# Blocks 2 and 3 of a fp32 RWKV kernel: the time norm on transposed tokens, and block 0's first v mix after its r mix

## The chip, the cores and the metric

The kernel runs on one core of one Trainium2 chip. The metric is the device time of one execution in microseconds (us), lower being better. One core has five engines that matter here: TensorE (PE, matrix products and transposes), VectorE (DVE), ScalarE (ACT), GpSimd (POOL, which here mostly issues DMA transfers) and SyncE (SP, which only issues DMA transfers). A transfer is issued by an engine's queue, in order, and lands some us later.

## The reference

2048 tokens of 512 features, fp32, pass through an RWKV block and then a gated FFN. Cut to what matters:

```python
x = x + attn(_layernorm(x))            # attn is the block below
# in the block, on its own input x:
h  = _layer_norm(x, ln1_g, ln1_b)
hh = _time_shift(h)                    # the token before
k = (h * tm_mk + hh * (1 - tm_mk)) @ Wk.T
v = (h * tm_mv + hh * (1 - tm_mv)) @ Wv.T
r = (h * tm_mr + hh * (1 - tm_mr)) @ Wr.T
x = x + sigmoid(r) * wkv(k, v, tm_first) @ Wo.T
h = _layer_norm(x, ln2_g, ln2_b)       # then the channel mix:
x = x + sigmoid((mixed by cm_mr) @ Wcr.T) * (silu((mixed by cm_mk) @ Wkey.T) @ Wval.T)
# outside the block:
x = x + ((silu(gate) * up) @ w_down.T) # gate, up from _layernorm(x) @ w_gate_up.T
```

The scan starts from an empty state for all tokens at once, so `wkv` is elementwise here. Two norms stand one behind the other ahead of k, v and r (the outer one and ln1); both come from the same mean and variance.

## The kernel before

**Tiling.** Tokens are worked in four blocks (`NB`) of 512 (`TB`), block 0 first. A token tile is 128 tokens on the partitions by 4x512; its turned form hT has features on the partitions, four chunks of 128 features by 512 tokens, plus one column for the token before the block. Products use halves of 256 tokens and, except those listed in `PLAIN` (L658, `plain_unit`), a Strassen scheme of seven products in place of eight (L556, `unit`): each needs sums of the operand's quarters (`sums_of`, DVE) and of the weight's quarters. A product's PSUM bank is copied out by ACT (accv at L576, u at L587, accx at L591) and added by DVE (`tt`, L385).

**Weight sums.** `prepare` (L144 to L160) loads four raw quarters by POOL's queue (L149), makes four sums with DVE (L385) and stores them to DRAM by POOL's queue (L160). `ring` (L163 to L165) loads each product's weight, raw or sum, by SP's queue into a ring of 12 tiles. A load made by `paced` waits for the latest matmul recorded before it, so that it isn't issued too early.

**The time norm.** `time_norm(b)` takes mean and variance per token on DVE (`moments`, L399 and L400), forms `rstd` and `both` (the scale of the two norms together), scales the tile to h (four DVE tensor_scalar, L389), transposes h by PE (`transposed`, 16 transposes at L441), and ACT evacuates each bank of four with ln1's gain and bias to hT (L453). Column 0 of hT is copied from `carry` before it and the last column saved after it (L449, L459). Block 0 has a version of its own, `first_block` (L810 to L844). `residual` (L742, ACT) makes the outer normalised x, which the block adds to.

**Mixes.** `mix` makes an operand of k, r or v from hT: per chunk ACT scales the shifted hT (L494) and DVE adds the scaled hT (L393); two shifted copies are made ahead of the first mixed one. The k product's results go through two ACT exponentials (L879, L880) and DVE (L389, L393).

**Order.** PE's, DVE's and ACT's instructions stand in the order in which the program records them. A planner does this recording: main programs such as `k_unit` and `up_unit` record the products one after the other, and between the products `tick` runs pieces of generators from two queues: of the front one of `hot` and the first three of `background`, the first that can go on is stepped until the time that its pieces are estimated to cost is spent. A `yield` ends a piece, and `yield 1` also waits for the next tick. A generator pushed with a condition starts when the condition holds; those behind it that have a condition then wait too. `later` puts a piece off by ticks. The order on SP and POOL is the tile framework's. `push_mix` (from L862) pushes a block's mixes with the condition that its norm is finished and an operand tile is free.

The main program (from L1270) begins:

```python
second_half = first_block()
for n in "rv":
    push_mix(0, n, time_mix(0, n))
credit[1] = 0.6
k_unit(0)
```

and, for each block b, records the gate product of its channel mix, then the out product of block b + 1, pushes `norm{b+2}`, and with the first `up_unit` of b pushes the mixes of block b + 2 and the channel norm of block b + 1. So the time norms of blocks 2 and 3 run beside products of blocks 0 and 1, at about 150 and 310 us.

Of the kernel before, what the change touches and what calls it, by code (L numbers as in the profile page):

```python
# [9 lines left out]
F32 = mybir.dt.float32  # L10
AF = mybir.ActivationFunctionType
ALU = mybir.AluOpType
# [3 lines left out]
P = 128  # L16
H = 512
NC = H // P
TB = 512
NT = TB // P  # L20
# [9 lines left out]
LN1G, LN1B, LN2G, LN2B, FIRST, MK, MV, MR, CK, CR = range(10)  # L30
NVEC = 10

WK, WV, WR, WO, WCR = range(5)

PLAIN = {(0, WK), (0, WR), (0, WV), (0, WO), (1, WK), (1, WR)}
WKEY = 5
WVAL = 9
# [23 lines left out]
def rwkv_ffn_kernel(  # L61
    ctx: ExitStack,
    tc: tile.TileContext,
    x: bass.AP,
    vecs: bass.AP,
    w: bass.AP,
    wd: bass.AP,
# [2 lines left out]
    nc = tc.nc  # L70
    ntok = x.shape[0]
    NB = ntok // TB
# [12 lines left out]
    dram = ctx.enter_context(tc.tile_pool(name="dram", bufs=1, space=bass.MemoryType.DRAM))  # L85
# [3 lines left out]
    htp = mixes.enter_context(tc.tile_pool(name="htp", bufs=2))  # L89
# [9 lines left out]
    def tok_tile(name):  # L99
        return tokp.tile([P, NT, H], F32, tag="tok", name=name)  # L100
# [103 lines left out]
    def cost(n, fixed=0.135, per=0.00107):  # L204
        spent[0] += max(0.17, fixed + per * n)
# [7 lines left out]
    def flush():  # L213
        while put_off:
            flush_one()
# [27 lines left out]
    finished = set()  # L243
# [68 lines left out]
    def push(name, gen, ready=None):  # L312
        background.append([ready, gen, name, False, background])
# [18 lines left out]
    ident = const.tile([P, P], F32, name="ident")  # L332
# [6 lines left out]
    pt = ps.tile([P, 2, HB], F32, tag="ps", name="warm")  # L339
# [27 lines left out]
    carry = {}  # L367
# [4 lines left out]
    def vcol(row, c):  # L372
        return vec[:, row, c : c + 1]
# [22 lines left out]
    def moments(src, mv):  # L396
        for t in range(src.shape[1]):
            st = small.tile([P, 6], F32, tag="st", name="st")
            nc.vector.bn_stats(st, src[:, t, :])  # L399
            nc.vector.bn_aggr(mv[:, t, :], st)  # L400
            cost(512)
            cost(0)
            yield

    def rsqrt(v, y, n, early=False):


        if early:
            nc.gpsimd.tensor_tensor(y, v, mhalf[:, :n], ALU.pow)
            for _ in range(n // NT):  # L410
                yield 1
            return
        a = small.tile([P, n], F32, tag=f"a{n}", name="a")
        yi = y.bitcast(I32)
        ts(yi, v.bitcast(I32), 1, None, ALU.logical_shift_right)
        ts(yi, yi, -1.0, float(0x5F3759DF), ALU.mult, ALU.add)
        yield
        for _ in range(3):
            stt(a, y, -0.5, y, ALU.mult, ALU.mult)
            tt(a, a, v, ALU.mult)  # L420
            stt(y, a, 1.5, y, ALU.add, ALU.mult)
            yield

    def scaled(src, dst, mv, rstd):
        for t in range(NT):
            ts(
                dst[:, t, :],
                src[:, t, :],
                mv[:, t, 0:1],
                rstd[:, t : t + 1],  # L430
                ALU.subtract,
                ALU.mult,
            )
            yield

    def transposed(h, evacuate):
        for c in range(NC):
            pt = bank()
            flat = pt.rearrange("p a b -> p (a b)")
            for t in range(NT):  # L440
                nc.tensor.transpose(  # L441
                    flat[:, t * P : (t + 1) * P], h[:, t, c * P : (c + 1) * P], ident
                )
            evacuate(c, flat)
            spent[0] += 0.4
            yield

    def shifted_norm(s, h, hT, g, b):
        nc.vector.tensor_copy(hT[:, :, 0:1], carry[s])  # L449
        cost(0)  # L450

        def evacuate(c, pt):
            nc.scalar.activation(  # L453
                hT[:, c, 1:], pt, AF.Identity, bias=vcol(b, c), scale=vcol(g, c)
            )

        yield from transposed(h, evacuate)
        yield 1
        nc.vector.tensor_copy(carry[s], hT[:, :, TB : TB + 1])  # L459
        cost(0)  # L460
# [11 lines left out]
    def op_free():  # L472
        return live_ops[0] < 3
# [236 lines left out]
    def product_of(b, n, name, sink, by_token, done=None, free=op_done):  # L710
        if (b, name) not in ops:
            flush()
        plain = (b, n) in PLAIN
        B = Lazy((b, name), plain)
# [18 lines left out]
    x1s, ops, hTs = {}, {}, {}  # L733

    def residual(b, xb, cols):

        x1 = tok_tile("x1")
        x1s[b] = x1
        for t, (mean, scale) in enumerate(cols):
            shift = small.tile([P, 1], F32, tag="shift", name="shift")  # L740
            stt(shift, mean, -1.0, scale, ALU.mult, ALU.mult)
            nc.scalar.activation(x1[:, t, :], xb[:, t, :], AF.Identity, bias=shift, scale=scale)  # L742
            spent[0] += 0.4
            yield

    def affine(var, mv):


        n = mv.shape[1]
        ts(var[:, :n], mv[:, :, 1], EPS, None, ALU.add)  # L750
        ts(var[:, n : 2 * n], mv[:, :, 1], 1.0 + EPS, EPS * EPS, ALU.mult, ALU.add)

    def time_norm(b):
        xb = xin.pop(b)
        mv = small.tile([P, NT, 2], F32, tag="mv", name="mv")
        yield from moments(xb, mv)
        var = small.tile([P, 2 * NT], F32, tag="var2", name="var2")
        affine(var, mv)
        two = small.tile([P, 2 * NT], F32, tag="two", name="two")
        yield from rsqrt(var, two, 2 * NT, b == 1)  # L760
        rstd, both = two[:, :NT], two[:, NT:]
        h = tok_tile("h")
        yield from scaled(xb, h, mv, both)
        hT = htp.tile([P, NC, TB + 1], F32, tag="hT", name="hT_a")
        hTs[b, "a"] = hT
        tails[b] = residual(b, xb, [(mv[:, t, 0:1], rstd[:, t : t + 1]) for t in range(NT)])
        if b == 1:
            yield 1
        yield 1
        yield from shifted_norm("a", h, hT, LN1G, LN1B)  # L770

    def first_block():

# [76 lines left out]
    tails = {}  # L850
# [7 lines left out]
    def time_mix(b, name):  # L858
        row, n = {"k": (MK, WK), "r": (MR, WR), "v": (MV, WV)}[name]
        yield from mix((b, name), hTs[b, "a"], row, (b, n) in PLAIN)  # L860

    def push_mix(b, name, gen):  # L862
        norm = f"normb{b}" if name in ("cr", "ck") else f"norm{b}"
        push((b, name, "t"), gen, lambda: norm in finished and op_free())

    qs = {}

# [38 lines left out]
    def v_unit(b):  # L906
# [5 lines left out]
        def done():  # L912
            hidden_sums((b, "g"), q, (b, WO) in PLAIN)

# [367 lines left out]
    for n in "rv":  # L1282
        push_mix(0, n, time_mix(0, n))
# [7 lines left out]
    for n in "krv":  # L1291
        push_mix(1, n, time_mix(1, n))
# [10 lines left out]
    for b in range(NB):  # L1303
# [9 lines left out]
        if nxt:  # L1313
            push(f"norm{b + 2}", time_norm(b + 2))
# [46 lines left out]
def _layout(inputs):  # L1361

    import numpy as np

    def get(name):
        return np.asarray(inputs["L0_" + name])

    x = np.ascontiguousarray(get("attn_x").reshape(-1, H))
    names = ["ln1_g", "ln1_b", "ln2_g", "ln2_b", "tm_first", "tm_mk", "tm_mv", "tm_mr", "cm_mk", "cm_mr"]
    vecs = np.stack([get("attn_" + n).reshape(NC, P).T for n in names], axis=1)  # L1370

    gu = get("ffn_w_gate_up")
    half = gu.shape[0] // 2
    gate, up = gu[:half], gu[half:]
    key, val, down = get("attn_Wkey"), get("attn_Wval"), get("ffn_w_down")
    blocks = [get("attn_" + n) for n in ("Wk", "Wv", "Wr", "Wo", "Wcr")]
    blocks += [key[j * H : (j + 1) * H] for j in range(4)]
    blocks += [val[:, j * H : (j + 1) * H] for j in range(4)]
    blocks += [gate[j * H : (j + 1) * H] for j in range(4)]
    blocks += [up[j * H : (j + 1) * H] for j in range(4)]  # L1380

    def quarter(m, i, j):
        q = m[i * HB : (i + 1) * HB, j * HB : (j + 1) * HB]

        return q.T.reshape(2, P, HB).transpose(1, 0, 2)

    w = np.stack(
        [
            np.stack([quarter(m, i, j) for i, j in ((0, 0), (0, 1), (1, 1), (1, 0))])
            for m in blocks  # L1390
        ]
    )
    def quarter_quarter(i, j, m, k):
        at = slice(i * HB + m * P, i * HB + (m + 1) * P)
        lo = j * HB + k * P

        q = [down[at, g * H + lo : g * H + lo + P].T for g in range(4)]
        return np.stack(q, axis=1).reshape(P, 4 * P)

    places = ((0, 0), (0, 1), (1, 1), (1, 0))  # L1400
    wd = np.stack(
        [np.stack([quarter_quarter(i, j, m, k) for m, k in places]) for i, j in places]
    )
    return {
        "x": x,
        "vecs": np.ascontiguousarray(vecs),
        "w": np.ascontiguousarray(w),
        "wd": np.ascontiguousarray(wd),
    }
# [19 lines left out]
```

## Time and profile before

| | |
|---|---|
| runs | 1241.83, 1241.83, 1243.77 us; median 1241.83 |
| the profiled execution | 1242.04 us, its span 1239.9 us |
| TensorE clock granted | 1.0 |
| PE busy by stretch (us of us) | 0 to 25: 22.45; 50 to 100: 50.00; 100 to 150: 49.59; 150 to 300: 150.00 |
| | 300 to 480: 180.00; 480 to 500: 19.80; 500 to 800: 300.00; 800 to 1240: 435.40 |
| DVE busy by stretch | 50 to 100: 38.16; 100 to 150: 37.48; 150 to 200: 36.59 |
| ACT busy by stretch | 50 to 100: 19.99; 100 to 150: 19.70; 150 to 200: 24.28 |
| share of DMA engines' time | 50 to 100: 0.72; 100 to 150: 0.88; 150 to 200: 0.68; 200 to 300: 0.86 |
| transposes of the norms (L441) | 16 records for a block's norm, 128x128 each, mean 0.27 us, at 150.7, 206.0, 309.6 and so on |

The profile is that of one execution, so its numbers are compared with its own time. A line of a timeline reads: start, length, engine, line, operation, output and inputs, count, and in brackets how long the engine had been idle and what ended that. A line of the waits reads: what waited, for whom, us in total, times, longest. A line of the windows reads: the stretch, then its length, and busy us and count of PE, PEld (weight loads), DVE, ACT and POOL, then PE's clock, the DMA share and GB/s. In the list of DMA issues the last column is us from issue to landing. The matmuls of PE overlap, so that a record is longer than the step from one to the next.

### The profile page before, as it was taken

How to read it: one execution, taken by the hardware profiler on the slowest of the kernel's cores; microseconds unless marked ns; L12 is line 12 of the kernel's file. 1: busy time of each engine (PE TensorE's matmuls, PEld its weight loads, DVE VectorE, ACT ScalarE, POOL GpSimd, SP SyncE). 2: the span in 40 equal slices, each digit the busy share in tenths (PEclk: the TensorE clock that was granted, in tenths of full speed). 3: DMA queues.
4: the chain of work that ended last, by engine and by line, in shares of the span. 5: the costliest groups of instructions: out<-in, count | busy, mean ns of one | idle time of the engine just before them, and what ended most of it. 6: DMA issues, size and time to landing. Idle time of an engine off the chain costs nothing.

```text
span 1239.9 us, 18124 instructions
## 1 busy us (share of the span) xinstructions
PE 1231.2 (99%) x6552; PEld 1105.0 (89%) x6552; DVE 704.8 (57%) x1307; ACT 356.9 (29%) x661; POOL 153.7 (12%) x278
## 2 busy tenths in 40 slices
PE   8999999999999999999999999999999999999998
PEld 7888888888888888888888888998899888998898
DVE  5877686487763758523542365556546365462466
ACT  5534352142631334212311232122221222112211
POOL 2232221222212222221100000000000000000000
PEclk9999999999999999999999999999999999999999
DMA  6768885898778887899756755895569845785576
GB/s 204 238 216 286 288 277 199 295 318 288 247 255 261 283 261 240 262 329 305 229 145 181 225 144 151 268 339 153 145 183 302 275 141 154 240 295 160 152 223 204
DMA packets 138983, 290.12 MB, mean 234 GB/s; under 512 B 17424, under 2 KB 18576, under 8 KB 137872
## 3 DMA queue, kind: packets, MB, share of 16 engines
q1 hardware_dynamic: 116448, 217.11, 57.4%
q0 software_dynamic: 21440, 70.27, 15.5%
q10 hardware_dynamic: 1008, 1.59, 0.3%
q8 instruction: 53, 0.87, 0.3%
q14 instruction: 34, 0.28, 0.1%
HBM read 246.96 MB, written 41.94 MB: 233 GB/s over the span
## 4 chain that ended last, share of the span: by engine, by line
PE 96%; ACT 1%; DVE 1%; DMA 1%; POOL 0%; issue 0%; DVEq 0%
PE ps L556 54%; PE ps L1160 14%; PE accv L556 11%; PE accx L556 11%; PE ps L658 6%; PE ps L441 1%; DMA raw<-in_wd 1%; ACT mix L494 0%; DMA x<-in_x 0%; ACT mix L823 0%; ACT hT_a L815 0%; DVE mix L393 0%; DVE resid L385 0%; DVE r L385 0%; POOL raw L149 0%
## 5 line engine op out<-in xcount | busy, mean ns | idle before, releaser
L556 PE MATMUL ps<-zT,w 128*128 128x256 f32 x1280 | 289.5, 379 | 0.0
L556 PEld LDWEIGHTS ps<-zT,w 128*128 128x128 f32 x1280 | 241.9, 190 | 32.2
L556 PE MATMUL ps<-mix,w 128*128 128x256 f32 x920 | 210.8, 379 | 0.2 <-ACT u L587 0.2
L556 PEld LDWEIGHTS ps<-mix,w 128*128 128x128 f32 x920 | 174.5, 190 | 24.2 <-ACT u L587 0.6
L385 DVE TENSOR_TENSOR u<-u,accx 128x512 f32<-128x512 f32 x66 | 45.2, 684 | 119.8 <-ACT accx L591 119.8
L1160 PE MATMUL ps<-w,hid 128*128 128x128 f32 x832 | 104.5, 275 | 0.0
L556 PE MATMUL ps<-w,t 128*128 128x256 f32 x456 | 102.3, 379 | 0.0
L1160 PEld LDWEIGHTS ps<-w,hid 128*128 128x128 f32 x832 | 99.8, 192 | 0.8
L556 PEld LDWEIGHTS ps<-w,t 128*128 128x128 f32 x456 | 86.4, 190 | 11.6
L1160 PE MATMUL ps<-w,quads 128*128 128x128 f32 x704 | 89.0, 275 | 0.4 <-ACT r L1172 0.4
L576 ACT COPY accv<-ps 128x512 f32<-128x512 f32 x66 | 37.6, 570 | 179.3 <-PE ps L556 179.3
L1160 PEld LDWEIGHTS ps<-w,quads 128*128 128x128 f32 x704 | 84.2, 192 | 0.9 <-ACT r L1172 0.5
L385 DVE TENSOR_TENSOR raw<-raw 128x512 f32<-128x512 f32 x92 | 63.1, 686 | 37.0 <-DMA raw<-in_wd 11.8
L591 ACT COPY accx<-ps 128x512 f32<-128x512 f32 x66 | 37.7, 571 | 156.9 <-PE ps L556 155.2
L385 DVE TENSOR_TENSOR u<-ps,u 128x512 f32<-128x512 f32 x66 | 45.5, 690 | 55.5 <-PE ps L556 55.2
L658 PE MATMUL ps<-mix,w 128*128 128x256 f32 x320 | 71.0, 380 | 2.1 <-DVE mix L393 2.0
L587 ACT COPY u<-ps 128x512 f32<-128x512 f32 x66 | 38.6, 585 | 112.0 <-PE ps L556 112.0
L1172 ACT COPY r<-ps 128x128 f32<-128x128 f32 x112 | 29.8, 266 | 142.1 <-PE ps L1160 142.1
L1254 POOL DMA_DIRECT2D out<-resid x12 | 8.6, 718 | 498.1 <-DVE resid L385 498.1
L658 PEld LDWEIGHTS ps<-mix,w 128*128 128x128 f32 x320 | 60.2, 190 | 11.0 <-DVE mix L393 3.1
L556 PE MATMUL accv<-zT,w 128*128 128x256 f32 x256 | 60.6, 379 | 0.0
L556 PE MATMUL accx<-zT,w 128*128 128x256 f32 x256 | 60.5, 379 | 0.0
(159 smaller groups left out, 1654.0 us busy)
## 6 DMA issues: line engine op xcount, KB each, us to landing
w<-sum SPq DMA_DIRECT2D x312, 256.0 KB, 3.3
w<-in_w SPq DMA_DIRECT2D x254, 256.0 KB, 3.7
w<-dd SPq DMA_DIRECT2D x112, 256.0 KB, 3.6
raw<-in_w POOLq DMA_DIRECT2D x48, 256.0 KB, 5.5
sum<-raw POOLq DMA_DIRECT2D x48, 256.0 KB, 4.3
w<-d SPq DMA_DIRECT2D x48, 256.0 KB, 3.5
q<-in_w POOLq DMA_DIRECT2D x36, 256.0 KB, 6.0
sum<-q POOLq DMA_DIRECT2D x36, 256.0 KB, 4.0
```

Source lines behind the costliest of these rows:

```text
L385: nc.vector.tensor_tensor(out, a, b, op)
L441: nc.tensor.transpose(flat[:, t * P : (t + 1) * P], h[:, t, c * P : (c + 1) * P], ident)
L556: mm = nc.tensor.matmul(pz[:, m, :], lhsT=lhsT, rhs=rhs, start=first and g == 0 and m == 0 and k == 0, stop=g == last and k == 1, skip_gro ...
L576: "z", A11, B11, True, pop_held, read=lambda: nc.scalar.copy(accv, acc["z"])
L587: nc.scalar.copy(tmp["u2"], acc["z"])
L591: nc.scalar.copy(accx, acc["z"])
L658: mm = nc.tensor.matmul(acc[i, j][:, m, :], lhsT=act[:, k, lo] if by_token else wg[:, k, lo], rhs=wg[:, k, :] if by_token else act[:, k, : ...
L1160: mm = nc.tensor.matmul(dst, lhsT=x[k][:, g, :], rhs=wt[:, g, :], start=first and g == 0, stop=g == 3, skip_group_check=True,)
L1172: nc.scalar.copy(st["r"][:, m, n * P : (n + 1) * P], st["z"])
L1254: eng.dma_start(out_t[b][:, tokens, cols], rs[b][:, tokens, cols])
```

## The change

Blocks 2 and 3 (`b >= TURNED`) no longer make h and transpose it. The host also hands in x turned (`xt`: block, feature in chunk, chunk, token), which is loaded as one transfer of 1 MB per block on SP's queue, paced. Mean and scale of the tokens, which stand as columns (128 x 4 each), are transposed by PE into one bank of 4 partitions by 256, copied out by ACT, stored to a small DRAM tile by ACT's queue, and loaded back after three ticks as two rows, each broadcast to 128 partitions (128x512, from 2 KB), again by ACT's queue. After three more ticks DVE subtracts the mean's row from each chunk of xT and multiplies by the scale's row, and ACT applies gain and bias from SBUF to hT. `residual` is queued as before, recorded a little earlier.

The second part is in `push_mix`: block 0's mix for v starts when that for r is finished, where it started when the norm was finished, so that their pieces alternated.

In the order of the built program PE has 32 transposes of 128x128 less and 4 with an output of 4x128 more; SP has two loads more; ACT has two stores and four row loads more; the pieces of the planner that follow on DVE, ACT and PE are shifted against the products to about 600 us, among them the transposes of the channel norms of blocks 1, 2 and 3, which come seven, four and two products later. POOL's order differs in one place (the store of a sum of weight 11 stands behind two raw loads).

```diff
@@ -32,6 +32,7 @@
 
 WK, WV, WR, WO, WCR = range(5)
 
+TURNED = 2
 PLAIN = {(0, WK), (0, WR), (0, WV), (0, WO), (1, WK), (1, WR)}
 WKEY = 5
 WVAL = 9
@@ -62,6 +63,7 @@
     ctx: ExitStack,
     tc: tile.TileContext,
     x: bass.AP,
+    xt: bass.AP,
     vecs: bass.AP,
     w: bass.AP,
     wd: bass.AP,
@@ -759,6 +761,9 @@
         two = small.tile([P, 2 * NT], F32, tag="two", name="two")
         yield from rsqrt(var, two, 2 * NT, b == 1)
         rstd, both = two[:, :NT], two[:, NT:]
+        if b >= TURNED:
+            yield from turned_norm(b, xb, mv, rstd, both)
+            return
         h = tok_tile("h")
         yield from scaled(xb, h, mv, both)
         hT = htp.tile([P, NC, TB + 1], F32, tag="hT", name="hT_a")
@@ -768,6 +773,51 @@
             yield 1
         yield 1
         yield from shifted_norm("a", h, hT, LN1G, LN1B)
+
+    stats = {
+        b: dram.tile([2, TB], F32, tag=f"stats{b}", name=f"stats{b}") for b in range(TURNED, NB)
+    }
+
+    def turned_norm(b, xb, mv, rstd, both):
+
+
+        xT = tok_tile("xT")
+        paced(nc.sync.dma_start(xT, xt[b]))
+
+        yield 1
+        pt = flat(bank())
+        for k, cols in enumerate((mv[:, :, 0], both)):
+            nc.tensor.transpose(pt[:NT, k * P : (k + 1) * P], cols, ident)
+        sb = flat(q_tile("row"))
+        nc.scalar.copy(sb[:NT, : 2 * P], pt[:NT, : 2 * P])
+        nc.scalar.dma_start(
+            stats[b].rearrange("s (t p) -> t s p", p=P),
+            sb[:NT, : 2 * P].rearrange("t (s p) -> t s p", s=2),
+        )
+        for _ in range(3):
+            yield 1
+        rows = []
+        for k in range(2):
+            r = flat(q_tile("row"))
+            nc.scalar.dma_start(r, stats[b][k : k + 1, :].broadcast_to([P, TB]))
+            rows.append(r)
+        tails[b] = residual(b, xb, [(mv[:, t, 0:1], rstd[:, t : t + 1]) for t in range(NT)])
+        hT = htp.tile([P, NC, TB + 1], F32, tag="hT", name="hT_a")
+        hTs[b, "a"] = hT
+        for _ in range(3):
+            yield 1
+        nc.vector.tensor_copy(hT[:, :, 0:1], carry["a"])
+        cost(0)
+        for c in range(NC):
+            tt(xT[:, c, :], xT[:, c, :], rows[0], ALU.subtract)
+            tt(xT[:, c, :], xT[:, c, :], rows[1], ALU.mult)
+            nc.scalar.activation(
+                hT[:, c, 1:], xT[:, c, :], AF.Identity, bias=vcol(LN1B, c), scale=vcol(LN1G, c)
+            )
+            yield
+        yield 1
+        nc.vector.tensor_copy(carry["a"], hT[:, :, TB : TB + 1])
+        cost(0)
 
     def first_block():
 
@@ -861,7 +911,9 @@
 
     def push_mix(b, name, gen):
         norm = f"normb{b}" if name in ("cr", "ck") else f"norm{b}"
-        push((b, name, "t"), gen, lambda: norm in finished and op_free())
+
+        alone = (0, "r") if (b, name) == (0, "v") else norm
+        push((b, name, "t"), gen, lambda: {norm, alone} <= finished and op_free())
 
     qs = {}
 
@@ -1366,6 +1418,8 @@
         return np.asarray(inputs["L0_" + name])
 
     x = np.ascontiguousarray(get("attn_x").reshape(-1, H))
+
+    xt = np.ascontiguousarray(x.reshape(-1, TB, NC, P).transpose(0, 3, 2, 1))
     names = ["ln1_g", "ln1_b", "ln2_g", "ln2_b", "tm_first", "tm_mk", "tm_mv", "tm_mr", "cm_mk", "cm_mr"]
     vecs = np.stack([get("attn_" + n).reshape(NC, P).T for n in names], axis=1)
 
@@ -1403,6 +1457,7 @@
     )
     return {
         "x": x,
+        "xt": xt,
         "vecs": np.ascontiguousarray(vecs),
         "w": np.ascontiguousarray(w),
         "wd": np.ascontiguousarray(wd),
```

## The prediction

> **What bounds the kernel now.** I read the page's first part, then what TensorE (PE) waits for, then the timelines around the edited places. The page:
>
> ```profile
> span 1239.9 us, 18124 instructions
> PE 1231.2 (99%) x6552; PEld 1105.0 (89%) x6552; DVE 704.8 (57%) x1307; ACT 356.9 (29%) x661; POOL 153.7 (12%) x278
> ```
>
> PE works 1231.2 of 1239.9 us. So an edit gains only what it takes off PE's stream, or out of PE's 8.7 us of idle time. PE's waits:
>
> ```profile
> PE ps L658 <- DVE mix L393: 2.0, 2, 1.1
> PE warm L341 <- POOL ident masks.py:199: 1.4, 1, 1.4
> PE ps L556 <- PE ps L556: 0.4, 1, 0.4
> PE ps L1160 <- ACT r L1172: 0.4, 1, 0.4
> PE ps L556 <- ACT u L587: 0.2, 1, 0.2
> ```
>
> Two waits are for block 0's first mixes. One is at 9.8 us, in `first_block`, which is untouched. The other is at 27.5, inside the stretch that `push_mix` changes. The rest of the idle time is the tail (last matmul ends 1231.57) and is untouched.
>
> **Removed: transposes.** In the chain of waits and in PE's timeline block 2's sixteen stand as
>
> ```profile
> 150.88 1.75 PE ps L441 x16
> 150.72 1.91 PE L441 MATMUL ps<-ident,h 128*128 128x128 f32 x16
> 309.62 1.47 PE L441 MATMUL ps<-ident,h 128*128 128x128 f32 x12
> 312.66 0.60 PE L441 MATMUL ps<-ident,h 128*128 128x128 f32 x4
> ```
>
> 1.75/16 = 0.109 us of path each. Blocks 2 and 3 lose 32: −3.50. No row shows the four new transposes (output 4x128). They still read 128 partitions, so I take the same 0.109 each, +0.44; bounds 0 and 0.44. Net −3.06 (to −3.50).
>
> The Trainium skill ("TensorE: Matmul & The Clock Gate", "Part 4: PE-mode transpose") says that a 128×128 transpose costs about 275 ns in a kernel, PE's access latency dominating. The records here last 0.27 us each, but the chain advances by 0.109; on the skill's figure 28 fewer would free an estimated 7.7 us.
>
> **Moved: v's first mix.** PE, ACT and DVE around the gap:
>
> ```profile
> 17.00 10.53 PE L658 MATMUL ps<-mix,w 128*128 128x256 f32 x48
> 28.43 17.93 PE L658 MATMUL ps<-mix,w 128*128 128x256 f32 x80 [0.90 <-DVE mix L393]
> ```
> ```profile
> 23.25 2.54 ACT L494 ACTIVATE mix<-hT_a,onem 128x512 f32<-128x512 f32 x4
> 25.70 0.61 ACT L879 ACTIVATE e<-r 128x512 f32<-128x512 f32 x1
> 26.34 0.63 ACT L880 ACTIVATE r<-r 128x512 f32<-128x512 f32 x1
> 26.88 2.54 ACT L494 ACTIVATE mix<-hT_a,onem 128x512 f32<-128x512 f32 x4
> ```
> ```profile
> 27.62 0.75 DVE L393 SCALAR_TENSOR_TENSOR mix<-hT_a,vec,mix 128x512 f32<-128x512 f32 x1 [2.22 <-ACT mix L494]
> 25.00:50.00 25.00, 23.97 (x114) 20.53 (x113) 20.43 (x45) 13.34 (x22) 11.13 (x17) 1.00 0.74 238
> ```
>
> Of ACT's first four shifted copies (L494) two are v's; r's third is the first of the second group, and DVE's mix of it starts at 27.62, 2.22 us idle. PE has used up k and r's first two chunks at 27.45 and starts again at 28.43; the window lacks 25 − 23.97 = 1.03. Without v's two copies (2 × 0.61) the e and r pair (L879) starts at 24.5 instead of 25.7, r's third copy runs from 25.7 to 26.3, and its mix of 0.75 ends near 27.1 instead of 28.37, 0.3 before PE wants it: the gap closes. If DVE had other work then, the mix would slip by one operation of 0.68 and half the gap would stay. v's mixes end near 34; PE needs them near 39.7. What is late next: block 1's transposes. Their last h ends at 45.95 now, near when PE arrives (46.2); PE comes about 1 us earlier, DVE's chain of e, q and h only about 0.5. I give back 0.1 (0 to 0.5): −0.9 (−0.5 to −1.03).
>
> **Added: the statistics' way.** (Times on the old clock; the new is some 1 us earlier from 28 on.)
> - xT: 1 MB on SP's queue, paced, issued near 142 and 301. The rows for 1 MB (7.2 and 6.8 us) put it near 149 and 308; SP itself loses some 0.3 us per issue. The weights queued behind it were asked for about 12 products (20 us) ahead of use and land in 3.3 to 3.7: cost 0.
> - Store, then two row loads on ACT's queue. An ACT-queue issue holds ACT for 0.45 (x) to 0.71 (w). Stat transposes at about 145.5 and 302.7, store about 147 and 304, rows issued about 151.5 and 311. The rows also wait for xT's landing (a shared semaphore), with some 2 us to spare.
>
> ```profile
> resid<-res SPq DMA_DIRECT2D x4, 1024.0 KB, 7.2
> w<-in_w ACTq DMA_DIRECT2D x4, 256.0 KB, 4.5
> vec<-in_vecs ACTq DMA_DIRECT2D x1, 20.0 KB, 5.4
> out<-resid SPq DMA_DIRECT2D x2, 64.0 KB, 1.6
> ```
>
>  The trace has no broadcast load from DRAM. By these rows a row lands in 1.6 to 7.2; I take 4.5 (same queue and size). DVE's first xT operation then waits until about 157 and 315.5. Behind it on DVE stand the sums of raw weights and u; behind ACT's hT stand the accv and accx copies that PE needs. In block 3 PE's product at 320.2 needs accv, whose copy is behind two hT: it is late once the second row takes over 6.2 us from its issue (7.2 in block 2). At 4.5: cost 0.
> - DVE: eight tensor_tensor (0.68 each, 5.4) for four tensor_scalar of 0.5 (2.0): +3.4 us a block. ACT's four hT stay, their source now SBUF. DVE makes it up in idle time: after block 2 it waits 2.13 us for PE at 194.18, and more in small gaps. Cost 0 there; with that cover gone it is the next item.
> - Reordering: block 1's channel norm transposes come seven products later, about 218.3, and wait for h, which follows raw sums:
>
> ```profile
> 212.05 1.42 DVE L385 TENSOR_TENSOR raw<-raw 128x512 f32<-128x512 f32 x2 [0.96 <-DMA raw<-in_w]
> ```
>
>  With raw landing about 210.3 as before, the chain of sums and h (8.5 us) ends at 218.9; PE wants the fourth h at 218.6. I take +0.3 (0 to 1.5). Block 2's and 3's have 1.5 and 4 us to spare: 0.
> - The 0.2 wait of L556 (u behind four mixes on ACT at 487.4) probably shifts away: −0.1 (0 to −0.2).
>
> **Sum.** −3.06 − 0.9 + 0.3 − 0.1 = −3.8 from the profiled execution's 1242.04 (span 1239.9 and 2.1 around it) gives 1238.3; that execution was 0.2 above the median of 1241.83, so 1238.1. Own range of this case: −4.7 to −1.9 less the 0.2: 1237.1 to 1239.9.
>
> **The rivals.**
> - *Rows land late* (ends slower). For: the longest landing in 186–206 us is 10.4, block 2 is in a stretch with 0.7 to 0.9 DMA share, 128 partitions read the same 2 KB, and 20 KB of vec took 5.4. Against: 256 KB on this queue took 4.5. At 10.4 PE stalls 10.4 − 6.2 = 4.2 in block 3 and 3.2 in block 2: +7.4 against −3.8 gives 1245.5. It decides as slower from about 9 us of landing in each.
> - *DVE late for block 1's channel norm* or for the weight sums after block 2: 3.4 us more DVE work lands in the burst of sums (SP waits 14.0 us for sum 12 already), h comes 2 us late instead of 0.3: 1239.8. For: three edits meet there. Against: DVE's 2.13 us idle at 194.
>
> ```profile
> DMA to landing us min/median/max: 2.3/6.4/10.4
> 194.18 0.69 DVE L385 TENSOR_TENSOR u<-ps,u 128x512 f32<-128x512 f32 x1 [2.13 <-PE ps L556]
> ```
> - *The start gap only moves*: DVE's e and r keep r's mix late, or block 1's transposes give all back. Only transposes count: 1239.0. Against: ACT ended the 2.22 idle, and its first copies are v's.
> - *Each transpose frees its 0.273 us record*: (32 − 4) × 0.273 = 7.6, +0.9: 1233.5. For: the record's length, nothing else. Against: sixteen in 1.75 us, followed at once by products. (The rule of the Trainium skill given above would lead here; the chain of waits does not bear it out.)
>
> **How the numbers follow.** A measurement tells 0.2% (2.5 us) from no change, so faster ends at 1239.3. Chances: forecast 0.54 (0.52 of it faster, 0.02 same), start gap only moves 0.12 (0.08 faster, 0.04 same), DVE late 0.13 (same), rows late 0.18 (0.13 slower, 0.05 same), long transposes 0.02 (faster), something unnamed 0.01 (slower). Faster 0.62, same 0.24, slower 0.14. Range 1236.9 to 1241.9: from the best end to about the old median, leaving out the slow cases above it and the long transposes.
>
> **What would show it.** Right: 28 fewer PE matmul records in all; no PE wait L658 at 27; PE 99% busy with 1228 us; between 140 and 330 us no new PE wait over 0.3 except at about 218, on h. Wrong: a PE wait on accv or accx copies near 169 or 320 with DVE idle on the row's DMA (rows late); waits on ring weights `w<-sum` after 180 (DVE late); a PE gap moved to 45 (start); four 4x128 transposes costing more than 0.44; the time outside the span changed.

## The result, and the profile after

The changed kernel takes 1239.05 us in the median of nine runs (1237.85 to 1239.45), against 1241.85 in nine runs of the kernel before beside them (1241.76 to 1243.77): a ratio of 0.9973, 95% interval 0.9964 to 0.9982. It is 2.8 us faster, just beyond the 0.2% that the prediction called measurable. The forecast was 1238.1, so about a quarter of the expected gain of 3.75 us is missing, and the runs spread over 1.6 us where nearly all runs of the kernel before lie within 0.4. Both are taken up below.

The profiled execution took 1239.38 us, its span is 1237.6 us. The page's first part (busy time, share of the span, count of instructions):

```profile
span 1237.6 us, 18092 instructions
PE 1228.9 (99%) x6524; PEld 1101.8 (89%) x6524; DVE 711.9 (58%) x1315; ACT 358.0 (29%) x663; POOL 153.1 (12%) x278
```

PE has 28 records less, as the change says, and DVE is 7.1 us busier. What PE waits for:

```profile
PE warm L343 <- POOL ident masks.py:199: 1.4, 1, 1.4
PE ps L660 <- DVE mix L395: 1.1, 1, 1.1
PE ps L860 <- DVE h L391: 0.9, 1, 0.9
PE ps L558 <- PE ps L558: 0.4, 1, 0.4
PE ps L1212 <- ACT r L1224: 0.4, 1, 0.4
PE ps L443 <- DVE h L391: 0.2, 1, 0.2
```

Of the two waits for mixes only block 0's first is left: the gap at 27 us is gone. The 0.2 of the kernel before on the u copy (L587) is gone too. New are 0.9 us for block 0's h at the very start (L860) and 0.2 for block 1's h at 47 us. The 0.9 costs nothing by itself: these transposes start at 8.26 us, in the kernel before at 8.34. PE's timeline around the edited places:

```profile
8.26 1.44 PE L860 MATMUL ps<-ident,h 128*128 128x128 f32 x8 [0.90 <-DVE h L391]
10.76 7.13 PE L660 MATMUL ps<-mix,w 128*128 128x256 f32 x24 [1.06 <-DVE mix L395]
17.73 1.04 PE L860 MATMUL ps<-ident,h 128*128 128x128 f32 x8
18.61 28.13 PE L660 MATMUL ps<-mix,w 128*128 128x256 f32 x128
46.58 0.49 PE L443 MATMUL ps<-ident,h 128*128 128x128 f32 x3
47.24 0.77 PE L443 MATMUL ps<-ident,h 128*128 128x128 f32 x5 [0.17 <-DVE h L391]
...
146.31 0.27 PE L790 MATMUL ps<-ident,mv 128*4 128x128 f32 x1
146.42 0.27 PE L790 MATMUL ps<-ident,two 128*4 128x128 f32 x1
146.53 1.89 PE L558 MATMUL ps<-mix,w 128*128 128x256 f32 x8
...
219.05 2.16 PE L443 MATMUL ps<-ident,h 128*128 128x128 f32 x16
```

The same places in PE's timeline of the kernel before:

```profile
10.84 5.45 PE L658 MATMUL ps<-mix,w 128*128 128x256 f32 x24 [1.06 <-DVE mix L393]
16.13 1.04 PE L810 MATMUL ps<-ident,h 128*128 128x128 f32 x8
46.20 1.04 PE L441 MATMUL ps<-ident,h 128*128 128x128 f32 x8
206.00 1.91 PE L441 MATMUL ps<-ident,h 128*128 128x128 f32 x16
```

Setting the same PE instruction of both traces side by side gives each term. The two stat transposes take 0.22 from 146.31 to 146.53. Block 1's sixteen at 219.05 take 0.25 longer than the 1.91 of the kernel before. The 128 products from 18.61 run without a break: from the second L860 group to block 1's transposes it is 28.85 us, 1.22 less than the 30.07 before (46.20 − 16.13).

| where | prediction | this execution against the one before |
|---|---|---|
| clock and waits at the start (second L860 group: 16.13 before, 17.73 now) | 0 | +1.60 |
| gap at 27 us, then block 1's first transposes | −0.9 | −1.22 + 0.39 = −0.83 |
| 32 transposes less, 4 more | −3.06 | 2 × (−1.75 + 0.22) = −3.06 |
| block 1's channel norm | +0.3 | +0.25 |
| the wait at 487 us and smaller things | −0.1 | −0.31 |
| last matmul's end (1231.57 before, 1229.22 now) | −3.8 | −2.35 |
| tail, and time outside the span (2.14 before, 1.78 now) | 0 | +0.05 − 0.36 |

All terms that the prediction had come out nearly as forecast. What is missing in this execution is one that it did not have: 1.6 us at the start, in instructions that the change doesn't touch.

The last row has a gain that was not forecast either. The time outside the span is 1.77 to 1.88 us in all nine runs; in the runs of the kernel before listed with the experiments it is 2.05 to 2.17. The prediction had named such a change as a sign against it. It seems to go with block 2: where only block 3 is turned (e11 below) it is 2.05 to 2.15. Its cause is not shown.

Back to the 1.6 us. Windows of PE's start (length; busy us and count of PE, PEld, DVE, ACT, POOL; granted clock, DMA share, GB/s):

```profile
4.40:7.70 3.30, 2.96 (x27) 2.76 (x25) 2.69 (x9) 0.00 (x0) 1.04 (x1) 1.00 1.05 378
7.70:11.10 3.40, 1.65 (x9) 1.18 (x10) 2.69 (x10) 1.95 (x5) 1.01 (x1) 0.99 1.05 389
11.10:14.40 3.30, 3.30 (x9) 2.65 (x8) 2.28 (x5) 2.01 (x5) 0.00 (x0) 0.50 0.77 286
```

From 11.1 to 14.4 us the granted clock is 0.50 and PE gets through 9 matmuls. In the kernel before it was 1.00 there, and the 24 products that took 7.13 us here took 5.45. Is this the change's doing or chance? And is it also what the other eight runs lack?

### The profile page after: what moved, and what is told of

Read it like the earlier page. It is cut to its first block, busy times and chain, and to the rows that moved or that the text cites. A ratio compares the mean times of both kernels' runs of the same rounds, so it can differ in the third digit from the quotient of the medians.

```text
span 1237.6 us, 18092 instructions
## 1 busy us (share of the span) xinstructions
PE 1228.9 (99%) x6524; PEld 1101.8 (89%) x6524; DVE 711.9 (58%) x1315; ACT 358.0 (29%) x663; POOL 153.1 (12%) x278
## 4 chain that ended last, share of the span: by engine, by line
PE 96%; DVE 2%; ACT 1%; DMA 1%; issue 0%; DVEq 0%
PE ps L558 54%; PE ps L1212 14%; PE accv L558 11%; PE accx L558 11%; PE ps L660 5%; PE ps L443 1%; DVE e L395 0%; DMA w<-in_w 0%; DVE mix L395 0%; DMA x<-in_x 0%; ACT mix L873 0%; ACT hT_a L865 0%; DVE q L387 0%; ACT mix L496 0%; DVE st L401 0%; DVE resid L387 0%
```

## The experiments

The twelve kernels were timed in four groups (e1 to e4, e5 to e8, e9 to e11, e12), each on another chip and with the kernel before beside it, whose median was 1241.87 to 1241.93 in all four. On the way "a dipped execution" means one with this half clock at the start.

### One part alone

`e1_mix_only` keeps the new rule for v's mix and turns no block; `e2_norm_only` turns blocks 2 and 3 and starts v's mix as before.

```diff
-TURNED = 2
+TURNED = 4
```
```diff
-        alone = (0, "r") if (b, name) == (0, "v") else norm
+        alone = norm
```

Expected of e1:

> Only the v mix waits; no block is turned (TURNED = 4). My theory (terms add up, and the start has a clock dip of 1.6 us that depends on the phase of the launch and not on the change): the gap at 27 us goes, some 0.2 is given back at block 1's transposes: 1241.85 - 1.06 = 1240.8 in executions without the dip, 1242.4 in those with it. Rival (the change itself brings the dip, through the turned norm's loads or the added input): all executions at 1240.8, since no turned norm runs here. Rival (the gap only moves): 1241.8.

Expected of e2:

> Only the turned norm; v's mix starts with r's as before. My theory: 28 transposes of 0.109 us less (-3.06), 0.25 lost at block 1's channel norm, 0.2 won at 487 us, the gap of 1.03 at 27 us stays: 1238.85 without the dip at the start, 1240.5 with it. Rival (the change itself brings the dip): all executions at 1240.5.

Measured: e1 1241.09 (1240.90 to 1242.77, 11 runs; ratio 0.9996, interval 0.9987 to 1.0004), eight runs at 1240.90 to 1241.22 and three at 1242.46 to 1242.77. e2 1238.91 (1238.13 to 1241.16, 11 runs; 0.9978, 0.9969 to 0.9986), nine at 1238.13 to 1239.55 and two above 1241. So the mix rule alone is worth some 0.8 us, and the turned norm some 3.0. Added up that is 3.9, but both together gave 2.8: on top of the turned norm the mix rule gained nothing in the median (1238.91 and 1239.05).

Each run also lists its mean granted clock. It is 0.998 in e1's three long runs and 0.999 or 1.0 in its other eight. It is 0.998 too in the five long runs of the kernel before whose clock is listed (1243.56 to 1243.63). Half a clock for 3.3 us of 1239 takes 0.0013 off the mean. So I take the 1.5 to 1.8 us by which these runs are longer for the dip, though none of them has a profile. It then comes without any turned norm, and without the change: the rival that the change brings it falls. Of the nine runs of the changed kernel only two list 0.998 (1239.38, which is the profiled one, and 1239.45). The other seven still have a median of 1238.97. The dip explains this profile, then, but not the median.

e2's runs are spread over 3 us with no 0.998 among them. Its profile (1239.22) shows a reason:

```profile
PE ps L660 <- DVE mix L395: 2.0, 2, 1.1
PE warm L343 <- POOL ident masks.py:199: 1.4, 1, 1.4
PE accv L558 <- ACT accv L578: 0.7, 1, 0.7
```

The third line is the wait that the prediction had as its rival "rows land late": PE's accv product in block 3 waits for ACT's accv copy, which stands behind two hT. (Of the two runs above 1241 there is no profile.)

### The start's idle time filled

Behind block 0's first eight transposes PE idles 1.06 us. `e3_after_fill` (the changed kernel) and `e4_before_fill` (the kernel before) put eight transposes of the identity there (`FILL` is 8), whose output nobody reads.

```diff
         mixed(0, two)
         for _ in two:
             pass
+        pt = bank()
+        for _ in range(FILL):
+            nc.tensor.transpose(pt[:, 0, 0:P], ident, ident)
```

Expected of e3:

> The changed kernel with eight idle transposes of the identity (8 x 0.109 = 0.87 us) recorded behind block 0's first eight transposes, where PE otherwise idles 1.06 us. My theory: PE is busy through the start in each phase, the clock stays at 1.0 from 11 to 14 us, and all executions come to 1237.8, spread below 0.5. Rival (the dip is not from PE's idle time at the start): median 1239.05 and a spread of 1.6 as in the changed kernel.

Expected of e4:

> The kernel before with the same eight idle transposes. My theory: nothing is won but the rare slow execution: 1241.85 in all, none at 1243.8. Rival (the idle time at the start costs time in itself): faster by 0.9, 1240.9.

Measured: e4 1241.89, all 11 runs between 1241.71 and 1242.00 (ratio 1.0, 0.9991 to 1.0008): as expected, no long execution, no clock of 0.998, and nothing else changed. Eleven runs show little by themselves, since without the fill only six of the 87 times of the kernel before are long. But none of the 45 runs with a filled start and no stall of several us (e3, e4, and e9, e11 and e12 below) lists 0.998, against 11 dipped ones among the 118 unfilled (the six long ones of the kernel before, two of the changed kernel, three of e1, none of e2). Chance alone would give that about once in 40 times.

e3 1238.59 (1237.41 to 1239.21, 7 runs; 0.9973, 0.9962 to 0.9984). Here my expectation was wrong: the spread stayed at 1.8 us and the median came only a third of the way from 1239.05 to 1237.8. No run lists 0.998, so something else varies. PE's timeline of e3:

```profile
217.34 0.38 PE L444 MATMUL ps<-ident,h 128*128 128x128 f32 x2
218.48 2.10 PE L444 MATMUL ps<-ident,h 128*128 128x128 f32 x14 [0.76 <-DVE h L392]
220.41 3.62 PE L559 MATMUL ps<-w,s 128*128 128x256 f32 x16
```

PE now waits for block 1's h, which in the dipped profile of the changed kernel cost 0.25. From the first of these transposes to the next product it is 3.07 us here (220.41 − 217.34), 2.00 there (221.05 − 219.05) and 1.74 in the kernel before (207.74 − 206.00), so the wait costs about 1.3. It also tells why the parts don't add up: in e2's profile, where the gap at 27 us is still there, PE reaches these transposes later than in e3, at 218.00, and leaves them earlier, at 220.11. In these two profiles, what the mix rule had won is spent waiting here. DVE's timelines of e3 and of the changed kernel say where h was:

```profile
210.62 1.42 DVE L388 TENSOR_TENSOR raw<-raw 128x512 f32<-128x512 f32 x2 [3.75 <-DMA raw<-in_w]
...
217.88 1.00 DVE L392 TENSOR_SCALAR h<-x,mv,rstd 128x512 f32<-128x512 f32 x2
```
```profile
211.27 1.42 DVE L387 TENSOR_TENSOR raw<-raw 128x512 f32<-128x512 f32 x2 [2.68 <-DMA raw<-in_w]
...
218.53 1.00 DVE L391 TENSOR_SCALAR h<-x,mv,rstd 128x512 f32<-128x512 f32 x2
```

In both, a raw sum of WK stands ahead of h in DVE's queue and waits for its loads. POOL's first issue of them is at 198.81 in e3 and at 200.52 in the changed kernel, 1.71 apart as PE is; the sums start only 0.65 apart. So the transfers, more than their issue, set this time: an undipped PE is 1.7 us earlier, and 1.07 of that (1.33 − 0.26) it spends waiting at 218 us. The dip and this wait partly stand in for each other: a dipped execution of the changed kernel is hardly longer than an undipped one that waits for h.

### A first repair that went wrong

If h should not stand behind WK's raw sums, keep the planner from recording weight sums (`prep_one`) while block 1's channel norm is under way:

```diff
-            if preps and not hot and credit[0] >= 1 and prep_one():
+            if preps and not hot and not hold[0] and credit[0] >= 1 and prep_one():
...
+        hold[0] = b == 1
         yield from moments(x1, mv)
...
         yield from scaled(x1, h, mv, rstd)
+        hold[0] = False
```

`e5_fill_hold` is e3 with this. `e6_rows_early` and `e7_rows_late` also move the row loads by a tick, the ticks after them adjusted so that PE's order stays (shown for e6; e7 has 4 and 2):

```diff
-        for _ in range(3):
+        for _ in range(2):
             yield 1
         rows = []
...
-        for _ in range(3):
+        for _ in range(4):
             yield 1
         nc.vector.tensor_copy(hT[:, :, 0:1], carry["a"])
```

`e8_three_blocks` is e6 with `TURNED = 1`.

Expected of e5:

> e3_after_fill, with the planner kept from recording weight sums on DVE between the first statistics of block 1's channel norm and its fourth h, so that h stands ahead of the raw sums that wait for their loads. My theory now (what is left over the predicted 1237.8 are PE's waits for that h, 0.2 to 1.1 us, and for block 3's accv copy behind the rows, 0 to 0.7, both varying with how long DMA takes): the wait on h goes, 1238.6 becomes 1237.8 in the median, and only the accv wait still varies, all within 1237.4 to 1238.4. Rival (the spread is from the clock or from weights that land late): 1238.6 and a spread of 1.8 as in e3_after_fill.

Expected of e6:

> e5_fill_hold with the two row loads recorded one tick (one product, 1.73 us) earlier in the same order of everything else. If rows land on the edge of what PE tolerates, as I now think: no wait on accv or accx, 1237.5 with a spread below 0.5. Rival (rows have slack, as I predicted with 4.5 us of landing): as e5_fill_hold.

Expected of e7:

> e5_fill_hold with the two row loads one tick later (1.73 us), the rest the same. Rows on the edge: PE waits in block 3 by 1.4 to 2.4 for the accv copy behind hT, and less or nothing in block 2: 1239.2 to 1240.2. Rival (1.7 us of slack, by the predicted 4.5 us of landing): as e5_fill_hold, no wait on accv.

Expected of e8:

> e6_rows_early with block 1 turned too (TURNED = 1). 14 transposes less again: -1.5, 1236.0, if block 1's hT is there when its first mixes are wanted at about 62 us. Rival: its rows land at about 55 and DVE's eight operations, 5.4 us, come while DVE is busiest; then PE waits for the mixes, 1 to 4 us, 1237 to 1240.

Measured: 1253.27 (e5, 4 runs, ratio 1.0087, 1.0074 to 1.01), 1254.00 (e6, 4 runs, 1.0095, 1.0082 to 1.0108), 1253.37 (e7, 5 runs, 1.0086, 1.0073 to 1.0099), 1249.86 (e8, 6 runs, 1.0058, 1.0044 to 1.0072). PE's timeline of e5:

```profile
211.33 3.75 PE L560 MATMUL ps<-w,t 128*128 128x256 f32 x8 [9.49 <-DMA w<-sum]
```

The last two sums of the weight before WK were held too. Their store and the load behind it on SP came late, PE stood still for 9.5 us, and the eight matmuls after that took 3.75 in place of 1.89. Neither expectation had this: the hold was mine, and it says nothing of rows. e6 and e7 carry the same stall (9.3 and 8.7), so they don't answer their question. e8 has other stalls, 3.9 for an e of DVE and 3.4 for u copies the largest. Its block 1 rows, issued at 48.07, are first used at 55.20 and 56.95, and the e that PE waits 3.9 for stands on DVE behind the operations that use them (60.22). That is more than the 1.5 that a block's transposes free. But e8 carries the hold and the earlier rows too, so no run shows what turning block 1 is worth by itself.

### The repair made narrower

`e9_h_first` holds back WK's sums only (against e5, only the part of the condition that differs):

```diff
-not hold[0] and credit[0] >= 1
+not (hold[0] and preps[0][0] == WK) and credit[0] >= 1
```

Expected of e9:

> e3_after_fill, with only the sums of WK (the raw sums that stand ahead of block 1's h) kept off DVE until the fourth h is recorded; the sums of the weight before it, whose lateness cost PE 9.5 us in e5_fill_hold, keep their place. If PE's wait on h is what the changed kernel loses beyond its accv wait: no wait of L444's transposes at 218 us, median 1237.8, between 1237.4 and 1238.4. Rival (WK's sums are then late in turn): a wait on a weight sum between 260 and 300 us, 1238.6 or more.

Measured: 1241.10 (1240.11 to 1241.80, 11 runs; 0.9993, 0.9984 to 1.0001). The wait on h is gone, and the rival came true. PE's largest new wait there (two more, on ACT's copies, are 0.8 and 0.2):

```profile
284.60 1.97 PE L560 MATMUL accv<-w,e 128*128 128x256 f32 x8 [1.72 <-issue]
```

and DVE's:

```profile
276.83 1.42 DVE L389 TENSOR_TENSOR raw<-raw 128x512 f32<-128x512 f32 x2 [3.91 <-issue]
...
283.81 0.69 DVE L389 TENSOR_TENSOR e<-u,e 128x512 f32<-128x512 f32 x1
```

The 1.72 us that the waits put down to "issue" end 0.1 us after an e that PE multiplies by (283.81 + 0.69 = 284.50). That e is behind raw sums that stood idle until 276.83; the chain of waits leads from them back to a `raw<-in_w` transfer. WK's sums, moved back, pushed the next weight's loads and sums back, and those waited in front of something else that PE wanted. I read this as the same wait moved. That is argued: no run took it away by itself.

### Rows one tick late, and block 3 alone

On e3's base, where PE's order and DVE's stay as they are, `e10_rows_late` repeats e7's edit, and `e11_block3_only` has `TURNED = 3`.

Expected of e10:

> e3_after_fill with the two row loads recorded one tick later (1.73 us) and the wait after them one tick shorter, so that PE's order and DVE's are the same. Rows on the edge of what PE tolerates: PE waits in block 3 for the accv copy by 1.2 to 2.4 us, and may wait a little in block 2, 1239.8 to 1241. By the predicted 4.5 us of landing there would be 1.7 us of slack and no wait: 1238.6.

Expected of e11:

> e3_after_fill with block 2 as before and only block 3 turned (TURNED = 3). Block 1's channel norm then keeps its old place ahead of the raw sums. By the terms: 1241.85 - 1.06 (start) - 14 x 0.109 = 1.53, and 0 to 0.7 for the accv copy: 1239.3 to 1240.0, no wait on h at 218. So turning block 2 would be worth 1.53 less its wait on h of 0.2 to 1.1.

Measured: e10 1239.74 (1238.33 to 1245.92, 12 runs; 0.9986, 0.9978 to 0.9995), at the lower edge of what I expected but far from no change: 1.15 above e3, and its runs reach 6.7 higher. e11 1239.94 (1239.66 to 1240.65, 11 runs; 0.9984, 0.9976 to 0.9993), as expected. Block 1's channel norm stands at 204.93 us there, ahead of the raw sums, and its sixteen transposes take 1.91 without a wait. So turning block 2 is worth 1.35 (1239.94 − 1238.59) of its 1.53.

The profile of e10 is of one of its long runs (1242.53). PE, and then windows around it:

```profile
321.28 3.50 PE L559 MATMUL accv<-mix,w 128*128 128x256 f32 x8 [2.57 <-ACT accv L579]
```
```profile
318.70:321.30 2.60, 0.03 (x2) 0.02 (x1) 2.56 (x5) 2.09 (x4) 0.00 (x0) 0.93 0.93 330
321.30:324.00 2.70, 2.70 (x6) 2.17 (x7) 2.53 (x5) 1.79 (x3) 0.00 (x0) 0.50 0.06 21
```

A wait of 2.57 for accv is followed by 2.7 us at half clock, and eight matmuls take 3.50 in place of 1.89: the stall costs 4.2 in all. The same bill followed the 9.5 us of e5.

The prediction said that accv is late in block 3 once the second row takes over 6.2 us from its issue. The timelines of five profiles test it (the second issue taken 0.43 behind the first; "used" is DVE's first operation that waits for the second row):

| kernel | second row issued | used | us | over 6.2 | PE's wait on accv |
|---|---|---|---|---|---|
| e3 | 309.46 | 315.71 | 6.25 | 0.05 | 0 |
| e11 | 309.54 | 316.31 | 6.77 | 0.57 | 0.43 |
| e2 | 309.16 | 316.20 | 7.04 | 0.84 | 0.69 |
| e12 (below) | 308.28 | 315.86 | 7.58 | 1.38 | 1.24 |
| e10 | 310.55 | 317.88 | 7.33, and issued 1.6 later | 2.7 | 2.57 |

(In e10 the row issue stands 1.67 us behind the start of ACT's s of accv, in the other four 0.08.) The changed kernel's own profile has no such wait: its first row is used at 315.61, 5.9 us after its issue, and the second one without a further stop. Its list of DMA issues gives for the rows of both blocks

```profile
row<-stats ACTq DMA_DIRECT2D x4, 256.0 KB, 6.3
```

The limit holds to within 0.2 us. What was wrong was the landing: 4.5 was taken, and in these five profiles the second row is usable after 6.25 to 7.6.

### The norm taken up earlier

In the planner's queue block 1's channel norm stands behind block 2's k mix, residual and r mix, and only three are looked at. `e12_norm_second`, on e3's base, pushes it ahead of the r mix and holds nothing back:

```diff
                 if nxt:
                     push_mix(b + 2, "k", time_mix(b + 2, "k"))
                     push_residual(b + 2)
-                    push_mix(b + 2, "r", time_mix(b + 2, "r"))
                 if b + 1 < NB:
                     push(f"normb{b + 1}", channel_norm(b + 1))
                 if nxt:
+                    push_mix(b + 2, "r", time_mix(b + 2, "r"))
                     push_mix(b + 2, "v", time_mix(b + 2, "v"))
```

Expected of e12:

> e3_after_fill with the channel norm of the block before pushed ahead of the r mix of the turned block, so that the planner takes it up two places earlier: block 1's four h then stand ahead of WK's raw sums, and no sum is held back (the sums of the weight before keep their place, unlike in e5_fill_hold, and WK's are recorded about as before, unlike in e9_h_first). If PE's wait on h was what was left, it goes: 1237.8 in the median, 1237.3 to 1238.5 with the accv wait's variation. Rival (each shift of the raw sums opens another wait, as in e9_h_first): 1239 or more, with a PE wait on an ACT copy or on e behind a raw sum between 220 and 300 us.

Measured: 1237.70 (1237.17 to 1239.01, 5 runs; 0.9966, 0.9952 to 0.9979), the lowest median here: 4.2 us below the kernel before and 1.35 below the changed kernel. DVE's and PE's timelines and PE's waits, of its longest run (1239.01):

```profile
201.31 1.92 DVE L392 TENSOR_SCALAR h<-x,mv,rstd 128x512 f32<-128x512 f32 x4
...
209.50 1.42 DVE L388 TENSOR_TENSOR raw<-raw 128x512 f32<-128x512 f32 x2 [2.41 <-issue]
```
```profile
205.39 0.60 PE L444 MATMUL ps<-ident,h 128*128 128x128 f32 x4
209.28 1.47 PE L444 MATMUL ps<-ident,h 128*128 128x128 f32 x12
```
```profile
PE accv L559 <- ACT accv L579: 1.2, 1, 1.2
PE ps L861 <- DVE h L392: 0.9, 1, 0.9
```

All four h are done at 203.2, ahead of the raw sums, and PE takes them without a wait. What remains is the wait on accv, whose 1.24 is nearly the distance from this run to the expected 1237.8.

This execution also shows what the filled start does. PE waits 0.9 for the first h here too, as in the dipped execution of the changed kernel. The same windows, of e12:

```profile
4.40:7.70 3.30, 3.04 (x27) 2.85 (x26) 2.65 (x8) 0.00 (x0) 1.03 (x1) 1.00 1.06 386
7.70:11.10 3.40, 2.38 (x17) 1.99 (x18) 2.73 (x10) 1.86 (x4) 0.97 (x2) 1.00 1.05 383
11.10:14.40 3.30, 3.30 (x16) 2.91 (x16) 2.28 (x5) 2.10 (x5) 0.06 (x1) 1.00 0.75 281
```

PE was busy 2.38 of 3.40 us in place of 1.65, and the clock stayed at 1.00. The two executions also begin alike. The 24 transposes that open PE's stream, of the changed kernel and of e12:

```profile
1.36 4.21 PE L343 MATMUL warm<-ident 128*128 128x128 f32 x24 [1.36 <-POOL ident masks.py:199]
1.36 4.29 PE L344 MATMUL warm<-ident 128*128 128x128 f32 x24 [1.36 <-POOL ident masks.py:199]
```

In the kernel before they take 5.33, and PE has no wait for the first h. So the length of this first stretch differs by the execution, and e12 is close to the one that dipped; with the gap filled it did not dip.

## Why the prediction was right, and what it missed

The range (1236.9 to 1241.9) and the side were right; the range is wide, though, and reaches up to no change. The forecast itself was 0.95 too low. The miss would be about 0.3 larger without the time outside the span, which fell and was not forecast.

- **The transposes.** Right to the hundredth: 0.109 us of path each, and 0.11 for the small ones (0.22 for a block's two, so 0.44 in all). The rival that counted each record's 0.27 us, and with it the rule of the Trainium skill ("TensorE: Matmul & The Clock Gate", "Part 4: PE-mode transpose") as an estimate of path time, falls: sixteen fewer freed 1.75, not 4.4.
- **The start gap.** Right: −0.83 in the profile against −0.9, and 0.8 by e1. Block 1's h is late next, as said (0.39; taken as 0.1, bound 0.5).
- **DVE's 3.4 us more a block.** Right: no new PE wait between 150 and 218 us in the changed kernel's profile.
- **Block 1's channel norm.** The mechanism and place were right (h behind raw sums that wait for their loads; eight products later by the traces, where the prediction has seven), the size was not: +0.3 fits the dipped execution (0.25), but an undipped PE comes earlier to transfers that do not, and pays about 1.3 (e3). The bound of 1.5 held.
- **The rows.** The mis-sized term. The way to the stall and its limit of 6.2 us were right, the 4.5 us of landing, taken from another transfer on the same queue, was too short. There were warnings. The trace had no broadcast load at all, and of the rows around it 20 KB in small pieces took 5.4, 1 MB took 7.2, and x's 256 KB loads on SP's queue 5.8. A term at zero with 1.7 us of cover over an unmeasured landing should have entered the sum with a share of a stall. It cost 0 in the profiled executions of the changed kernel and of e3, and 0.4 to 1.2 in those of e2, e11 and e12; for the changed kernel's other runs it is not known. The sign that the prediction gave for late rows, a PE wait on accv near 320 with DVE idle on the row, is in these three. The rival's ending, slower than before, did not come, and no profile of these kernels has the wait in block 2.
- **The start itself.** Missing altogether. The sum compared two executions as if untouched code took the same time in both. A dip of 1.6 us against a sum of 3.8 is a matter of each execution: six of the 87 times of the kernel before listed beside all these runs lie 1.65 to 1.92 above its median, the others at most 0.3.
- **Two sums.** The own range's upper end is −3.06 − 0.5 + 1.5 = −2.06 by its own terms, not −1.9. And late rows would reach 2.5 us above the old median only from about 9.9 of landing in each block (2 × 9.9 − 13.4 − 3.8), not from 9. Neither moves the forecast.

So of the 0.95 us that the median is above the forecast, the waits on h and on accv seem the larger part: e12, which takes the wait on h away and has the start filled, comes to 1237.70. This is argued from e2, e3 and e12; no undipped execution of the changed kernel itself has a profile. Whether v's new rule makes the dip more frequent stays open too: 0.998 is listed by two of the changed kernel's nine runs and three of e1's eleven, against none of e2's eleven and six long ones of the kernel before's 87. That leans towards yes, on few runs.

## What to carry to other kernels

A kernel that keeps its bottleneck engine 99% busy gains what is taken off that engine, but an engine that arrives earlier also meets waits that were just covered; look for transfers that do not move with it. Two gains measured apart need not add up for the same reason. Where an operation that waits for a load is recorded ahead of urgent work on the same engine, as the raw sums ahead of h on DVE, that work waits too: holding the waiting work back cost 2.5 (e9) and 15 (e5) against e3, while pulling the urgent work forward (e12) took the wait away. The 0.9 us by which e12's median is lower is less sure, since its five runs overlap e3's seven. Judge a change of a few us by several executions of each part, not by one profile, and look at the clock of the first microseconds before explaining a difference by the change.

## What was not expected of the hardware

- PE's clock fell to 0.50 for 3.3 us after 3.4 us in which PE was busy for 1.65, around two gaps of 0.90 and 1.06 us, and did not fall after 3.4 us with 2.38 busy (e12). The Trainium skill ("TensorE: Matmul & The Clock Gate", "Part 1: The HAM clock gate (the "warmup" mystery)") tells of a free-running window of 3413 ns that decides between half and full rate. The length agrees with the 3.3 us here, and a free-running window would explain why some executions dip and others of the same kernel don't; no run here shows the window itself. The Trainium skill's advice to avoid gaps over about 3 us (same page, "Why this matters for your kernels") would not have been enough here: the half rate came after two gaps of about 1 us, and after one of 2.57 (e10).
- A broadcast load of 256 KB, each partition reading the same 2 KB from DRAM, was usable 6.25 to 7.6 us after its issue in block 3, while the plain 256 KB weight loads by SP's queue took 3.4 to 3.8 in the median of the whole run of the changed kernel. The plain 256 KB loads of x by SP's queue took 6.3 there, so it is not shown that the broadcast makes the rows slow.
- Around 200 to 212 us, e3's PE was 1.71 us earlier than the dipped one, and the sums of the raw loads began only 0.65 earlier.
